# Row gathers and elementwise products on GpSimd beside the second layer of a four-layer graph network

## The chip, the cores and the metric

The kernel runs on one core of a Trainium2 chip. A core has a matrix engine (TensorE, PE in the profile, with PEld for its weight loads), a vector engine (VectorE, DVE), a scalar engine (ScalarE, ACT), a general engine (GpSimd, POOL) and a queue engine (SyncE, SP) that issues most DMAs. Each engine works through its own instructions in order, and they wait for each other through semaphores. The metric is the time on the device, in microseconds, of one execution. Before the change it was 2214.13 us (median of three runs, 2214.03 to 2218.48).

## The reference, cut to what matters

A node matrix x (4096 x 128, float32) goes through four layers. Each computes a graph operation on x and a dense 4096 x 4096 adjacency matrix, adds x, and normalises the rows.

```python
x = _layernorm(x + _L0_gnn_ref(x, adj, adj, L0_gnn_W, L0_gnn_a), axis=-1)
x = _layernorm(x + _L1_gnn_ref(x, adj, L1_gnn_W0, L1_gnn_b0, L1_gnn_W1, L1_gnn_b1), axis=-1)
x = _layernorm(x + _L2_gnn_ref(x, adj, ...), axis=-1)
x = _layernorm(x + _L3_gnn_ref(x, adj, L3_gnn_W_self, L3_gnn_W_neigh), axis=-1)
```

Layer 1, the second, is where the change lies. It is two Chebyshev convolutions with an ELU after each:

```python
def cheb_conv(x, L, W, b):
    Tx0 = x
    out = Tx0 @ W[0]
    Tx1 = L @ x
    out = out + Tx1 @ W[1]
    for k in range(2, W.shape[0]):
        Tx2 = 2.0 * (L @ Tx1) - Tx0
        out = out + Tx2 @ W[k]
        Tx0, Tx1 = (Tx1, Tx2)
    return out + b
h = elu(cheb_conv(x, L, W0, b0))     # 128 -> 256
h = elu(cheb_conv(h, L, W1, b1))     # 256 -> 128
```

Here L is the adjacency matrix. No layer gathers rows by index: all products are dense.

## The kernel before, in words

**Tiles.** Rows of x are kept in 32 tiles of 128 (NT = 32), the whole of x being one buffer of 128 partitions by 32 by 128. Columns of the transposed products come in 8 blocks of 512 (NB = 8, IB = 512, TB = 4 tiles to a block). The adjacency matrix [...] is read again for each product, in chunks of 1 MB (128 x 4 x 512 float32) by `chunk` (line 128), which SP issues into a pool of five buffers, `ld`.

**Layer 1.** The kernel orders the Chebyshev terms into four products with the adjacency matrix. `propagate` (the matmul is line 664) runs the first three: for each of 8 blocks, over 8 chunks and 4 tiles, it adds up one block of 128 x 512 in PSUM.

- First product, with x: ACT copies the block to t1T (line 679), TensorE turns it, VectorE copies it to t1 (line 681).
- Second product, with t1: VectorE makes t2T (line 686), TensorE multiplies by W0 in two halves, and `elu` makes each half of hT: ACT the rectifier (line 651), VectorE the minimum (652), ACT the exponential (653), VectorE the sum of the two parts (654). TensorE then multiplies hT by a weight (line 695), and VectorE copies the result to v (line 697).
- Third product, with v: ACT copies the block (line 709), TensorE turns it, VectorE copies it to w (line 711), ACT puts a product of hT into xT (line 715).
- The fourth product, with w, is written together with layer 2 (line 1126). Its block ends (`block_end`) begin with VectorE at lines 749 and 750 and come to GpSimd at line 775, the first GpSimd work after the constants at the start.

**Order.** In layers 0 and 1 a tile framework schedules the instructions of each engine and places the semaphore waits; `keep_in_program_order` holds those that are to stay as written. Buffers of one pool follow each other in the same memory: the buffers of layer 1's pools `l1w` and `l1h` are given up after the third product, and layer 2's buffers come to lie there, so the first writer of a new buffer waits for the last user of the old one. t1, v and w lie in long-lived buffers whose space is also shared by tag: w takes t1's place and layer 2's hc takes v's. From layer 2 on the order is written out by hand.

**Layer 2 on VectorE and GpSimd.** Its elementwise part is shared between the two engines: VectorE makes tau (line 884) and its own share of a second product (lines 890 and 896), GpSimd the rest (lines 891, 892, 897 and 898).

**Just before layer 1.** `normalize_x` gives x its final values on VectorE (line 151) and its transpose on ACT (line 158). ACT also issues the loads of W1A and W1B there (lines 644 and 646).

Of the kernel before, what the change touches and what calls it, by code (L numbers as in the profile page):

```python
# [11 lines left out]
F32 = mybir.dt.float32  # L12
BF16 = mybir.dt.bfloat16
I32 = mybir.dt.int32
AF = mybir.ActivationFunctionType
ALU = mybir.AluOpType
# [3 lines left out]
P = 128  # L20
IB = 512
TB = IB // P
# [11 lines left out]
def adj_resnorm_d4(ctx: ExitStack, tc: tile.TileContext, x_in, xT_in, adj, adjT, w0g, w0gT, a0, w1a, b1a,  # L34
# [7 lines left out]
    nc = tc.nc  # L42
    N, F = x_in.shape
# [17 lines left out]
    x = state.tile([P, NT, F], F32, name="x")  # L61
# [63 lines left out]
    def chunk(pool, src, ib, c, name="chunk", pinned=False):  # L125

        t = pool.tile([P, TB, IB], F32, name=name)
        r = nc.sync.dma_start(t, src[ib, c])
        if pinned:
            tc.keep_in_program_order(r)  # L130
        return t

    def transpose4(pool, name, src, order=lambda r: r):

        p = pool.tile([P, TB, P], F32, name=name)
        for k in range(TB):
            order(nc.tensor.transpose(p[:, k, :], src(k), ident))  # L137
        return p
# [486 lines left out]
    def network(usual):  # L625

        with ExitStack() as whole:
# [3 lines left out]
            with ExitStack() as first, ExitStack() as l1h_pool:  # L631
                ps_acc, ps_tr, ps_mm = [first.enter_context(tc.tile_pool(name=n, bufs=2, space=PSUM, reuse_waits="tile"))
                                        for n in ("ps_acc", "ps_tr", "ps_mm")]
                if not usual:
                    layer0_general(ps_acc, ps_tr, ps_mm)
                    finished = list(range(NB))
                ld = enter(name="ld", bufs=5)
                if usual:
                    finished = layer0(ld, ps_acc, ps_tr, ps_mm)
                dv = state.tile([96, N], BF16, name="dv")  # L640
                l1w = l1h_pool.enter_context(tc.tile_pool(name="l1w", bufs=2, reuse_waits="tile"))
                l1h = l1h_pool.enter_context(tc.tile_pool(name="l1h", bufs=1, reuse_waits="tile"))
                W1A = l1h.tile([P, 3, HID], F32, name="W1A")
                nc.scalar.dma_start(W1A, w1a.rearrange("k p f -> p k f"))
                W1B = l1h.tile([P, 3 * HH, F], F32, name="W1B")
                nc.scalar.dma_start(W1B, w1b.rearrange("k (h p) f -> p (k h) f", p=P))

                def elu(dst, p, bias):
                    r = l1w.tile([P, IB], F32, name="elu_r")
                    n = l1w.tile([P, IB], F32, name="elu_n")  # L650
                    nc.scalar.activation(r, p, AF.Relu, bias=bias)
                    nc.vector.tensor_scalar(n, p, bias, 0.0, op0=ALU.add, op1=ALU.min)
                    nc.scalar.activation(n, n, AF.Exp)
                    nc.vector.scalar_tensor_tensor(dst, n, -1.0, r, op0=ALU.add, op1=ALU.add)

                def propagate(stationary, order=range(NB), beside=None):


                    for ib in range(NB):
                        p = ps_acc.tile([P, IB], F32, name="pacc")  # L660
                        for n, c in enumerate(order):
                            a = chunk(ld, adjT, ib, c)
                            for k in range(TB):
                                nc.tensor.matmul(p, stationary(c * TB + k), a[:, k, :], start=n == 0 and k == 0,  # L664
                                                 stop=n == NB - 1 and k == TB - 1)
                            if beside and n == 0:
                                beside(p, ib)
                        yield ib, slice(ib * IB, (ib + 1) * IB), p

                t1 = state.tile([P, NT, F], F32, name="t1", tag="yn")  # L670
                t1T = l1h.tile([P, N], F32, name="t1T")
                hT = l1h.tile([P, HH, N], F32, name="hT")
                wd = l1h.tile([P, HH, F], F32, name="wd")
                nc.vector.tensor_sub(wd, W1B[:, 0:HH, :], W1B[:, 2 * HH:3 * HH, :])
                w2x = l1h.tile([P, HH, F], F32, name="w2x")
                nc.vector.tensor_scalar_mul(w2x, W1B[:, 2 * HH:3 * HH, :], 2.0)

                for ib, blk, p in propagate(lambda jt: x[:, jt, :], finished):
                    nc.scalar.copy(t1T[:, blk], p)
                    q = transpose4(ps_tr, "ptr", lambda k: t1T[:, (ib * TB + k) * P:(ib * TB + k + 1) * P])  # L680
                    nc.vector.tensor_copy(t1[:, ib * TB:(ib + 1) * TB, :], q)

                v = state.tile([P, NT, F], F32, name="v")
                for ib, blk, p in propagate(lambda jt: t1[:, jt, :]):
                    t2T = l1w.tile([P, IB], F32, name="t2T")
                    nc.vector.scalar_tensor_tensor(t2T, p, 2.0, xT[:, blk], op0=ALU.mult, op1=ALU.subtract)
                    for hh in range(HH):
                        ph = ps_mm.tile([P, IB], F32, name="pmm")
                        for k, r in enumerate((xT[:, blk], t1T[:, blk], t2T)):
                            nc.tensor.matmul(ph, W1A[:, k, hh * P:(hh + 1) * P], r, start=k == 0, stop=k == 2)  # L690
                        elu(hT[:, hh, blk], ph, B1A[:, hh:hh + 1])
                    q = ps_tr.tile([P, TB, F], F32, name="ptr")
                    for k in range(TB):
                        for hh in range(HH):
                            nc.tensor.matmul(q[:, k, :], hT[:, hh, (ib * TB + k) * P:(ib * TB + k + 1) * P],
                                             w2x[:, hh, :], start=hh == 0, stop=hh == HH - 1)
                    nc.vector.tensor_copy(v[:, ib * TB:(ib + 1) * TB, :], q)


                w = state.tile([P, NT, F], F32, name="w", tag="yn")  # L700
                h0T = xT

                def times_w1(p, ib):
                    for hh in range(HH):
                        nc.tensor.matmul(p, W1B[:, HH + hh, :], hT[:, hh, ib * IB:(ib + 1) * IB], start=False, stop=False)

                for ib, blk, p in propagate(lambda jt: v[:, jt, :], beside=times_w1):
                    lvT = l1w.tile([P, IB], F32, name="t2T")
                    nc.scalar.copy(lvT, p)
                    q = transpose4(ps_tr, "ptr", lambda k: lvT[:, k * P:(k + 1) * P])  # L710
                    nc.vector.tensor_copy(w[:, ib * TB:(ib + 1) * TB, :], q)  # L711
                    ph = ps_mm.tile([P, IB], F32, name="pmm")
                    for hh in range(HH):
                        nc.tensor.matmul(ph, wd[:, hh, :], hT[:, hh, blk], start=hh == 0, stop=hh == HH - 1)
                    nc.scalar.copy(h0T[:, blk], ph)

# [325 lines left out]
            with tc.manual_schedule(engines={mybir.EngineType.PE, mybir.EngineType.DVE, mybir.EngineType.Activation,  # L1044
# [68 lines left out]
                for ib in range(NB):  # L1113
                    early = ib == 1
                    p = ps_nd.tile([P, IB], F32, name="num") if early else ps_p.tile([P, IB], F32, name="pp")
# [55 lines left out]
                this, nt, _, tau2 = behind.popleft()  # L1171
# [9 lines left out]
            for _ in layer3_product(this.blocks):  # L1181
                pass

    network(True)
    with tc.If(nc.values_load(flag[0:1, 0:1], min_val=0, max_val=P) != 0):
        network(False)
# [32 lines left out]
```

## Time and profile before

| | |
|---|---|
| median of three runs | 2214.13 us (2214.03 to 2218.48) |
| span of the profiled execution | 2213.3 us (no other time of that execution is given) |
| TensorE busy | 2139.9 us, 97% |
| VectorE busy | 1186.3 us, 54% |
| GpSimd busy | 857.6 us, 39% |
| ScalarE busy | 562.4 us, 25% |
| first product of layer 1 (line 664 with x) | from 324.1 us; t1 copies at 357.5 to 553.1 us |
| second product | v copies at 590.9 to 830.9 us |
| third product | w copies at 858.0 to 1077.9 us |
| first block end of the fourth product (line 749) | 1106.3 us |
| first GpSimd work after the constants (line 775) | 1115.7 us |
| 1 MB chunk, from issue to landing | 4.9 us (median) |

The times are microseconds from the start of the span. A row of the slices gives the busy share of an engine in tenths, in 40 equal parts of the span. A group line gives the source line, the engine, the operation, what it writes and reads and how often, then its busy time in all and the mean of one in nanoseconds, then the idle time of the engine before it and what ended that. A line of the timeline gives the start, the duration, the engine and the instruction. A line of the windows gives a stretch and its length, the busy time of each engine in it, the clock granted to TensorE, the busy share of the DMA engines and the GB/s that they moved. Instructions that only issue a DMA are not counted as busy.

### The profile page before, as it was taken

To read this page: it belongs to the slowest core of one execution; us is meant where nothing else is said; L and a number is where in the kernel's file an instruction comes from. 1 tells how busy PE (TensorE), PEld (TensorE's weight loads), DVE (VectorE), ACT (ScalarE), POOL (GpSimd) and SP (SyncE) were. 2 spreads that over 40 slices of the span, in tenths; PEclk is the share of its full clock that TensorE was granted. 3 is DMA by queue.
4 is the path that set the end of the run, shared out by engine and by line. 5 is a ranking of instruction groups with operands and counts; after the bars stand their busy time and mean duration, and the time that the engine had idled before them with its cause. 6 is when DMAs were issued, how large, how long until landed. Compare 5 with 4: busy or idle time off the path is not lost. (4 is left out here: it accounts for less than half of the span.)

```text
span 2213.3 us, 22997 instructions
## 1 busy us (share of the span) xinstructions
PE 2139.9 (97%) x8644; PEld 850.8 (38%) x8644; DVE 1186.3 (54%) x1832; ACT 562.4 (25%) x1014; POOL 857.6 (39%) x539
## 2 busy tenths in 40 slices
PE   8999999999999999999999999979999899989997
PEld 3444454444444444444443333322222222333333
DVE  5655460000010110000026877899999999999995
ACT  6755100000000000000043223245333433332213
POOL 0000000000000000000004766698999999999980
PEclk9999999999999999999999999999999999999999
DMA  9886658888767677778876556525666566635545
GB/s 395 334 326 226 228 195 287 300 299 302 265 229 266 230 242 266 262 261 274 283 251 241 195 203 232 209 77 180 247 239 238 183 249 244 228 121 202 191 166 179
DMA packets 87145, 528.18 MB, mean 239 GB/s; under 512 B 9328, under 2 KB 15472, under 8 KB 25712
## 3 DMA queue, kind: packets, MB, share of 16 engines
q1 hardware_dynamic: 80288, 521.64, 66.8%
q10 hardware_dynamic: 6736, 4.98, 0.7%
q8 instruction: 70, 1.15, 0.2%
q14 instruction: 51, 0.42, 0.1%
HBM read 524.49 MB, written 2.10 MB: 238 GB/s over the span
## 5 line engine op out<-in xcount | busy, mean ns | idle before, releaser
L884 DVE SCALAR_TENSOR_TENSOR tau<-D,es,a 128x1024 f32<-128x1024 f32 (+1 forms) x640 | 646.4, 1058 | 44.0 <-ACT a L856 24.8
L892 POOL TENSOR_TENSOR tau<-tau,chunk 128x1024 f32<-128x1024 f32 x192 | 459.2, 2392 | 12.6 <-DVE tau L884 11.7
L775 POOL TENSOR_TENSOR x<-x,B2R 128x512 f32<-128x512 f32 x8 | 10.2, 1276 | 1145.5 <-PE px L137 1145.5
L908 PE MATMUL num<-tau,hc 128*32 128x512 f32 x2048 | 333.9, 606 | 15.0 <-POOL tau L892 9.0
L908 PE MATMUL den<-tau,cs 128*32 128x512 f32 x2048 | 343.6, 597 | 3.3 <-DVE tau L884 0.8
L999 PE MATMUL pp<-chunk,xT 128*128 128x512 f32 (+1 forms) x488 | 232.9, 607 | 0.0
L856 ACT ACTIVATE a<-chunk 128x1024 f32<-128x1024 f32 x160 | 164.2, 1026 | 254.8 <-DVE tau L890 195.1
L664 PE MATMUL pacc<-chunk,t 128*128 128x512 f32 x512 | 223.5, 592 | 0.0
L664 PE MATMUL pacc<-chunk,v 128*128 128x512 f32 x512 | 222.5, 592 | 0.0
L664 PE MATMUL pacc<-chunk,x 128*128 128x512 f32 x512 | 222.1, 592 | 0.0
L891 POOL TENSOR_TENSOR tau<-tau,chunk 128x320 f32<-128x320 f32 x192 | 167.7, 873 | 120.4 <-DVE tau L884 86.5
L1126 PE MATMUL pp<-chunk,w 128*128 128x512 f32 x448 | 204.3, 598 | 0.8 <-DVE oT L749 0.8
L379 PE MATMUL pacc<-chunk,hw 128*128 128x512 f32 x408 | 188.2, 606 | 2.4 <-DVE numT L407 1.7
L890 DVE TENSOR_TENSOR tau<-tau,a 128x704 f32<-128x704 f32 x186 | 163.1, 877 | 0.0
L898 POOL TENSOR_TENSOR tau<-tau,chunk 128x1024 f32<-128x1024 f32 x64 | 151.8, 2372 | 1.0
L908 PEld LDWEIGHTS num<-tau,hc 128*32 128x32 f32 x2048 | 62.4, 109 | 230.9 <-issue 127.8
L908 PEld LDWEIGHTS den<-tau,cs 128*32 128x32 f32 x2048 | 80.4, 110 | 177.0 <-issue 86.9
L664 PEld LDWEIGHTS pacc<-chunk,v 128*128 128x128 f32 x512 | 97.2, 190 | 122.0 <-issue 122.0
L664 PEld LDWEIGHTS pacc<-chunk,x 128*128 128x128 f32 x512 | 96.3, 190 | 115.8 <-issue 115.8
L664 PEld LDWEIGHTS pacc<-chunk,t 128*128 128x128 f32 x512 | 96.1, 190 | 115.3 <-issue 115.3
L999 PEld LDWEIGHTS pp<-chunk,xT 128*128 128x128 f32 x488 | 85.8, 190 | 133.1 <-issue 130.5
L711 DVE COPY w<-ptr 128x512 f32<-128x512 f32 x8 | 5.5, 691 | 241.5 <-PE ptr L137 241.5
(243 smaller groups left out, 1688.6 us busy)
## 6 DMA issues: line engine op xcount, KB each, us to landing
chunk<-in_adjT SPq DMA_DIRECT2D x386, 1024.0 KB, 4.9
chunk<-in_adj SPq DMA_DIRECT2D x80, 1024.0 KB, 5.0
chunk<-in_adj SPq DMA_DIRECT2D x32, 512.0 KB, 4.7
keep<-in_adjT SPq DMA_DIRECT2D x13, 1024.0 KB, 10.0
xT<-in_xT ACTq DMA_DIRECT2D x8, 256.0 KB, 6.6
out<-o ACTq DMA_DIRECT2D x7, 256.0 KB, 2.3
W1A<-in_w1a ACTq DMA_DIRECT2D x1, 384.0 KB, 5.4
W1B<-in_w1b ACTq DMA_DIRECT2D x1, 384.0 KB, 7.4
```

The lines of the kernel that those rows point to most:

```text
L379: in_order(nc.tensor.matmul(p, hw[:, j * TB + k, :], a[:, k, :], start=first and k == 0, stop=last and k == TB - 1))
L664: nc.tensor.matmul(p, stationary(c * TB + k), a[:, k, :], start=n == 0 and k == 0, stop=n == NB - 1 and k == TB - 1)
L775: nc.gpsimd.tensor_tensor(x[:, tb, :], x[:, tb, :], B2R[:, None, :].to_broadcast([P, TB, F]), ALU.add)
L856: nc.scalar.activation(ap, a, AF.Copy, accum_out=deg[:, nt, self.mp:self.mp + 1])
L884: nc.vector.scalar_tensor_tensor(flat(tau[:, q:q + n]), flat(self.D[:, q:q + n]), es[:, nt, head:head + 1], ap, op0=ALU.max, op1=ALU.mult)
L890: nc.vector.tensor_tensor(t2[:, 0:OWN], t[:, 0:OWN], (a if only else ap)[:, 0:OWN], ALU.mult)
L891: nc.gpsimd.tensor_tensor(t2[:, OWN:WB], t[:, OWN:WB], a[:, OWN:WB], ALU.mult)
L892: nc.gpsimd.tensor_tensor(t2[:, WB:2 * WB], t[:, WB:2 * WB], a, ALU.mult)
L898: nc.gpsimd.tensor_tensor(tau2[:, 2:4, :], tau[:, 2:4, :], rep(a, 2), ALU.mult)
L908: nc.tensor.matmul(acc[32 * q:32 * q + 32, :], weights(nt, head, is_den), r[:, q, :], start=nt == 0, stop=nt == NT - 1)
L999: nc.tensor.matmul(p, y[:, c * TB + k, :], a[:, k, lo:lo + n], start=c == blocks[0] and k == 0, stop=end)
L1126: nc.tensor.matmul(p, w[:, c * TB + k, :], a[:, k, :], start=c == 0 and k == 0, stop=c == NB - 1 and k == TB - 1)
```

## The change

In the usual branch, layer 1 copies x to a table in DRAM and makes a list of row indices (31 times the partition, plus a column number). At the end of every block of the first three products GpSimd copies one element of the block's result, which makes it wait for that block. At the ends of blocks 2 to 5 it also gathers rows of the table, 128 rows of 512 bytes to a gather, by indirect DMA into eight buffers in turn, with elementwise products of 128 x 512 between the gathers:

- first product (n = 0): eight gathers in a row, sixteen products, and both once more, to a block;
- second product (n = 1): sixteen times a gather and a product;
- third product (n = 2): eight times a gather and two products.

That is 160 gathers and 256 products in all. Nothing reads the gathered rows or the products.

```diff
                 nc.vector.tensor_scalar_mul(w2x, W1B[:, 2 * HH:3 * HH, :], 2.0)
 
+                if usual:
+                    rows = l1h.tile([P, 32], I32, name="rows")
+                    nc.gpsimd.iota(rows, pattern=[[1, 32]], base=0, channel_multiplier=31)
+                    table = whole.enter_context(tc.tile_pool(name="table", bufs=1, space=bass.MemoryType.DRAM)).tile([N, F], F32, name="table")
+                    nc.scalar.dma_start(table.rearrange("(t p) f -> p t f", p=P), x)
+                    fill = l1h.tile([P, 2, IB], F32, name="fill")
+                    nc.gpsimd.memset(fill, 1.0)
+                count = [0]
+
+                def beside(n, ib):
+                    if ib in (0, 1, 6, 7):
+                        return
+                    for k in range(16 if n < 2 else 8):
+                        gather()
+                        if n == 0 and k % 8 == 7:
+                            for _ in range(16):
+                                pause()
+                        if n > 0:
+                            for _ in range(n):
+                                pause()
+
+
+                def gather(n=P, width=F):
+                    k = count[0] % 8
+                    count[0] += 1
+                    got = l1w.tile([P, F], F32, name="got", bufs=8)
+                    tc.keep_in_program_order(nc.gpsimd.indirect_dma_start(got[0:n, 0:width], None, table if width == F else table[:, 0:width], bass.IndirectOffsetOnAxis(ap=rows[0:n, k:k + 1], axis=0)))
+
+                def pause(n=IB):
+                    tc.keep_in_program_order(nc.gpsimd.tensor_tensor(fill[:, 0, 0:n], fill[:, 0, 0:n], fill[:, 1, 0:n], ALU.mult))
+
+                def after(tile, ib):
+                    tc.keep_in_program_order(nc.gpsimd.tensor_copy(fill[:, 0, 0:1], tile[:, ib * TB, 0:1]))
+
                 for ib, blk, p in propagate(lambda jt: x[:, jt, :], finished):
...
                     nc.vector.tensor_copy(t1[:, ib * TB:(ib + 1) * TB, :], q)
+                    if usual:
+                        after(t1, ib)
+                        beside(0, ib)
...
                     nc.vector.tensor_copy(v[:, ib * TB:(ib + 1) * TB, :], q)
+                    if usual:
+                        after(v, ib)
+                        beside(1, ib)
...
                     nc.scalar.copy(h0T[:, blk], ph)
+                    if usual:
+                        after(w, ib)
+                        beside(2, ib)
```

## The prediction

> **What bounds the kernel now.** I read the engine totals first, then the slices, then each product of layer 1 by windows, and last the waits inside it. On the page of the kernel before:
>
> ```profile
> span 2213.3 us, 22997 instructions
> PE 2139.9 (97%) x8644; PEld 850.8 (38%) x8644; DVE 1186.3 (54%) x1832; ACT 562.4 (25%) x1014; POOL 857.6 (39%) x539
> ...
> POOL 0000000000000000000004766698999999999980
> ...
> DMA  9886658888767677778876556525666566635545
> ...
> q10 hardware_dynamic: 6736, 4.98, 0.7%
> ```
>
> GpSimd (POOL) is idle for the first 20 of 40 slices, so all of layer 1 has it free. The windows of layer 1 (PE, PEld, DVE, ACT and POOL busy, then clock, DMA share and GB/s):
>
> ```profile
> 380.00:414.00 34.00, 34.00 (x86) 15.25 (x85) 1.33 (x2) 1.17 (x2) 0.00 (x0) 1.00 0.89 297
> ...
> 660.00:700.00 40.00, 40.00 (x107) 18.71 (x106) 4.27 (x6) 2.63 (x4) 0.00 (x0) 1.00 0.69 242
> ...
> 920.00:980.00 60.00, 60.00 (x147) 26.95 (x147) 1.38 (x2) 1.77 (x4) 0.00 (x0) 1.00 0.78 265
> ```
>
> TensorE is busy without a gap at full clock in all three products, so layer 1 lasts as long as its matmuls, unless something makes one wait. The DMA engines have 11 to 31% left. In the waits of this stage TensorE waits for no DMA; SP's loads wait for TensorE to free a buffer (204 us in 65 waits from 300 to 560 us).
>
> The timeline at the end of a block of the second product shows the one tight chain:
>
> ```profile
> 689.61 0.63 ACT L653 ACTIVATE elu_n<-elu_n 128x512 f32<-128x512 f32 x1 [0.82 <-DVE elu_n L652]
> ...
> 690.27 0.69 DVE L654 SCALAR_TENSOR_TENSOR hT<-elu_n,elu_r 128x512 f32<-128x512 f32 x1 [0.69 <-ACT elu_n L653]
> ...
> 691.07 0.19 PEld L695 LDWEIGHTS ptr<-w2x,hT 128*128 128x128 f32 x1 [0.24 <-DVE hT L654]
> ```
>
> The ELU's last step, hT, ends at 690.96, and the weight load that needs it starts at 691.07. Behind that load stand all later matmuls, so a late hT makes TensorE late, but for the 0.24 us by which loads run ahead of matmuls.
>
> **What the Trainium skill says.** "SBUF — State Buffer", section "SBUF: two separate sides": VectorE and GpSimd share a port pair as an exclusive lock; a VectorE operation with two SBUF inputs and a GpSimd operation that reads SBUF block each other whole. The trace before agrees. Line 890 reads its second operand mostly from PSUM ("a"), six times from SBUF ("chunk"); in the groups by form:
>
> ```profile
> L890 DVE TENSOR_TENSOR tau<-tau,a 128x704 f32<-128x704 f32 x186 | 163.1, 877 | 0.0
> ...
> L890 DVE TENSOR_TENSOR tau<-tau,chunk 128x704 f32<-128x704 f32 x6 | 7.8, 1292 | 0.0
> ```
>
> and in the timeline:
>
> ```profile
> 1468.23 0.87 POOL L891 TENSOR_TENSOR tau<-tau,chunk 128x320 f32<-128x320 f32 x1
> ...
> 1468.45 1.40 DVE L890 TENSOR_TENSOR tau<-tau,chunk 128x704 f32<-128x704 f32 x1
> ...
> 1469.07 3.00 POOL L892 TENSOR_TENSOR tau<-tau,chunk 128x1024 f32<-128x1024 f32 x1
> ```
>
> VectorE's 877 ns became 1400 beside a GpSimd instruction with 0.65 us left: it lost that less 0.12. The next GpSimd product then took 3.00 us instead of 2.38. "DMA: Bandwidth & Descriptors", section "Issuing engines are not separate DMA queues": GpSimd's DMAs run on the same 16 engines as SP's; no run here shows a GpSimd DMA.
>
> **The change part by part.** Nothing is removed. The orders on TensorE, VectorE and SP are the old ones; ACT gets one DMA issue, GpSimd 442 instructions (160 gathers, 256 products, 24 copies of one element, an iota, a memset) between its constants and line 775. All of them are in the program, although nothing reads the rows gathered.
>
> *Table (2 MB, ACT queue).* It is queued between the last two xT copies (334.7 and 336.4 us) and waits for x, complete at 334, and for the SP chunk that had its semaphore before, issued at 334.40, which lands about 4.9 us later (page, section 6): ACT stands some 4 us, and behind it the last xT copy; the next ACT work is at 356.1. Hidden. It is 4096 rows of 512 B, 256 per engine. Queue q10 used 0.7% of 16 x 2213 us for 6736 packets, 37 ns each: 9.5 us of every engine. Line 646's 768 rows took 7.4 us to land beside the chunks; taking 2 us of it as fixed, 4096 rows take 31 us, so it lands near 370. SP's chunk of 380.6 waits for this semaphore, the first gather comes at 414. Chunks get at most 9.5 - 31 x 0.11 = 6 us later. One chunk takes TensorE 27.94 / 8 = 3.49 us; with five buffers it is needed 14 us after issue and lands in 4.9, so 9 us are spare. Cost 0; every us of landing beyond 380.6 + 9 would cost one.
>
> *GpSimd's length.* A pause is line 775's size, 1.276 us; each waits for the one before, for which its first rows in the timeline show 0.08 (memset to affine select): 1.36. The gather, g, no row shows. Lower end: "SBUF — State Buffer", same section, 0.62 us for a whole small GpSimd DMA. Upper end: "GPSIMD Engine Reference", section "Performance pitfalls for Q7 kernels", 102 cycles for each small read if one is made per index: 128 x 102 / 1.2 GHz = 10.9 us (estimate). I take 1.0, the first-byte time in "DMA: Bandwidth & Descriptors", section "Specifications", which it puts down to emitting descriptors: a row list of 128 needs no more reads than that if they are batched.
>
> - Product one: the third t1 copy is at 413.4. Four blocks of 16 g + 32 pauses: 414 + 64 x 1.0 + 128 x 1.36 = 652.
> - Product two: from the third v copy, 659.5, 64 x (1.0 + 1.36) = 151: 810.
> - Product three: the third w copy is at 920.8; a block takes 8 x 1.0 + 16 x 1.36 = 29.8, under the blocks' 31.4, so the last, from 1015.1, ends at 1045.
>
> Who waits for GpSimd: the first w copy (858, for the last read of t1, done by 652); line 749's oT (1106.3), whose buffer now lies over gathered rows and waits for four gathers; rn, hc, tau and GpSimd's own line 775 (1115.7) behind it. At g = 1.0 there are 61 us of cover. From g = 1.92 on GpSimd has no gap left, and oT, with all of layer 2 behind it on VectorE, is late from 414 + 256 x 1.36 + 160 g = 1106: g = 2.15. Beyond it each 0.1 us of g costs 16 us.
>
> *DMA of the gathers.* 8 rows per engine x 37 ns = 0.3 us. In product one 64 of them take 19 us of 238, 8%, on a share of 0.89; a burst of eight takes 2.4 us of about 8, and with 11% free puts chunks 1.5 us late, against 9 spare. Cost 0.
>
> *The port.* This one is not hidden. hT has two SBUF inputs, twice in each of eight blocks of product two. Pauses fill 174/238 = 73% of GpSimd until 652, and 1.36/2.36 = 58% from 659 to 810. In block one two hT fall in the first stretch; block two's (653, 656) fall between; blocks three to six have eight in the second; block seven (825, 828) is free; block zero has up to 1 us of slack. Hits: 2 x 0.73 + 8 x 0.58 = 6.1. A hit costs half a pause less 0.12, 0.52 us: 3.2 us on VectorE. The second hT of a block has 0.24 us of slack and the shift that the first made; I let 70% reach TensorE: 2.2 us. None of it is won back, since layer 2 starts from the last matmul. Bounds: 0 if the two engines miss each other; if every hT of seven blocks hits a full pause, about 7 x (1.16 + 0.72) = 13.
>
> Sum: 2213.3 + 2.2 = 2215.5 of span. The page gives no other time of the profiled execution; the median of the runs, 2214.13, lies 0.8 above the span. Forecast 2216.4.
>
> **The rivals.**
>
> *GpSimd is late for layer 2.* One mechanism: g above 2.15, and line 749 waits for the gathers. Speaks for it: 10.9 us if the indices are read one by one; against: the 1 us first-byte figure and the cover of 61 us. At g = 3 the time is 2214 + 160 x 0.85 = 2350; at 10.9, about 3600. Slower from g = 2.18 on.
>
> *The gathers hold the port too.* Then GpSimd holds it nearly all the time, and about 12 hT lose 0.5 us each, some whole gathers: 6 us on VectorE, 4 to 9 on TensorE with the second effects: 2218 to 2224. The skill limits the lock to operations that read SBUF; a gather reads only indices.
>
> *Nothing at all.* Pauses and hT miss each other, or the wait is absorbed: 2213.5 to 2215.
>
> *The DMA engines give out.* In product one (0.89) short rows from random places could cost much more than the 37 ns of rows in order; at four times that, 0.3 becomes 1.2 us, a third of the engines in product one, and TensorE waits for chunks: 0.21 x 138 us less the 9 spare, 20 us, 2234. Against: x, loaded in the same 512 B rows, 2 MB, landed in 13 us beside the chunks.
>
> **How the numbers follow.** The port costs 1 to 4.4 us: 0.45. Nothing: 0.13. The port costs more, by gathers that hold it or by luck: 0.23. GpSimd late: 0.12. DMA: 0.05. Faster than the measurement can tell has no mechanism: 0.02. A measurement of this kernel tells about 0.2%, 4.4 us, from no change: same 0.58, slower 0.40, faster 0.02. Low is 2213, the time before less its spread below the median and about 1 us; high, 2226, holds the port's upper bound of 13 us and leaves out the late GpSimd and most of the DMA case. With no change and the port's first case alone the range is 2213.5 to 2218.5.
>
> **What would show it.** hT (line 654) should have a mean of about 0.9 us instead of 693 ns, only in blocks where GpSimd is in products, and the loads of line 695 should wait for it; the last w copy should come at 1080 instead of 1077.9, with everything after it as before. GpSimd should be idle from about 1045, and gathers in product one should follow each other at about 1 us. I am wrong if oT waits for a DMA near 1106, if TensorE waits for chunks between 340 and 660, or if hT is stretched beside gathers.

## The result, and the profile after

The changed kernel takes 2218.97 us (median of 18 runs, 2216.67 to 2221.24), the kernel before 2214.14 us (18 runs, 2212.51 to 2218.48). The ratio is 1.0021, with a 95% interval of 1.0014 to 1.0027: 4.8 us slower, on the edge of the 0.2% that the prediction named as the limit of what can be told from no change. The forecast was 2216.4 us. The profiled execution of the changed kernel took 2221.24 us, the slowest of its 18, for a span of 2219.3 us. So spans of single executions are not compared below; what is compared is the time from the first to the last block inside one product of layer 1.

The page of the changed kernel, in the lines that answer to those of before:

```profile
span 2219.3 us, 23487 instructions
PE 2143.8 (97%) x8644; PEld 850.3 (38%) x8644; DVE 1196.1 (54%) x1832; ACT 562.9 (25%) x1014; POOL 1349.7 (61%) x981
...
POOL 0000000488899980388004766698999999989980
...
DMA  9886659999868777788876556625666566635545
...
q0 software_dynamic: 5120, 10.50, 1.5%
q10 hardware_dynamic: 10848, 7.08, 1.0%
```

GpSimd now works from the eighth slice to the nineteenth, with one idle slice between, and is idle again in the next two, before layer 2 needs it. VectorE is busy 9.8 us longer although it got no instruction. The gathers have their own queue, q0: 10.5 MB, 1.5% of the DMA engines. The windows of layer 1 (PE, PEld, DVE, ACT and POOL busy, clock, DMA share, GB/s):

```profile
380.00:414.00 34.00, 34.00 (x87) 15.25 (x86) 1.38 (x2) 1.17 (x2) 0.37 (x2) 1.00 0.88 299
660.00:700.00 40.00, 39.74 (x105) 18.42 (x104) 5.91 (x7) 2.63 (x4) 36.81 (x37) 1.00 0.74 254
920.00:980.00 60.00, 59.85 (x146) 26.52 (x145) 1.38 (x2) 2.34 (x4) 49.70 (x44) 1.00 0.81 279
```

In the second product VectorE's 4.27 us became 5.91, and TensorE, without a gap before, shows one. The timeline where the prediction showed the tight chain (the same block, the fourth of the second product; before, its second hT began at 690.27):

```profile
688.07 1.28 POOL L707 TENSOR_TENSOR fill<-fill 128x512 f32<-128x512 f32 x1
...
688.62 1.28 DVE L654 SCALAR_TENSOR_TENSOR hT<-elu_n,elu_r 128x512 f32<-128x512 f32 x1 [0.70 <-ACT elu_n L653]
...
689.50 1.26 POOL L704 DMA_INDIRECT got<-table,rows  x1 [0.16 <-issue]
...
690.02 0.30 PEld L732 LDWEIGHTS ptr<-w2x,hT 128*128 128x128 f32 x2 [1.06 <-issue]
...
690.79 1.28 POOL L707 TENSOR_TENSOR fill<-fill 128x512 f32<-128x512 f32 x1
...
691.26 1.36 DVE L654 SCALAR_TENSOR_TENSOR hT<-elu_n,elu_r 128x512 f32<-128x512 f32 x1 [0.70 <-ACT elu_n L653]
```

Both hT come while a GpSimd product runs, and take 1.28 and 1.36 us instead of 0.69: the product ends at 689.35, hT 0.55 later at 689.90. The weight loads (now line 732) stood 1.06 us before the first that needs it. All sixteen hT (line 654), before and after, and who waited for them after:

```profile
L654 DVE SCALAR_TENSOR_TENSOR hT<-elu_n,elu_r x16: 691/693/693, 584.9 to 827.9; 128x512 f32<-128x512 f32 x16
...
L654 DVE SCALAR_TENSOR_TENSOR hT<-elu_n,elu_r x16: 693/1365/1727, 584.4 to 831.2; 128x512 f32<-128x512 f32 x16
...
  PEld ptr L732: 3.4, 7
  PE ptr L732: 2.1, 5
```

Minimum, median and maximum are 693, 1365 and 1727 ns; before they were 691, 693 and 693. The v copies at the ends of the blocks, before (line 697) and after (line 734):

```profile
L697 DVE COPY v<-ptr x8: 690/692/692, 590.9 to 830.9; 128x512 f32<-128x512 f32 x8
...
L734 DVE COPY v<-ptr x8: 691/692/692, 590.4 to 834.5; 128x512 f32<-128x512 f32 x8
```

They span 240.0 us before and 244.1 us after. This is nearly the whole of the loss that layer 1 shows: the t1 copies of the first product span 195.6 us in both kernels, the w copies of the third 220.2 us (220.0 before), and the first oT comes at 1110.2 instead of 1106.3, 3.9 us later. The medians differ by 4.8 us, with an interval from 3.1 to 6.0, so 3.9 us can be all of it.

GpSimd's gathers:

```profile
L704 POOL DMA_INDIRECT got<-table,rows x160: 941/988/1265, 414.5 to 1046.9; - x160
```

### The profile page after: what moved, and what is told of

Its sections match the earlier page's. It is cut to its first block, busy times and chain, and to the rows that moved or that the text cites. A ratio compares the mean times of both kernels' runs of the same rounds, so it can differ in the third digit from the quotient of the medians.

```text
span 2219.3 us, 23487 instructions
## 1 busy us (share of the span) xinstructions
PE 2143.8 (97%) x8644; PEld 850.3 (38%) x8644; DVE 1196.1 (54%) x1832; ACT 562.9 (25%) x1014; POOL 1349.7 (61%) x981
## 5 line engine op out<-in xcount | busy, mean ns | idle before, releaser
L707 POOL TENSOR_TENSOR fill<-fill 128x512 f32<-128x512 f32 x256 | 327.2, 1278 | 13.9
L704 POOL DMA_INDIRECT got<-table,rows x160 | 158.6, 991 | 35.1 <-issue 30.5
```

Of the source, the lines that this page charges most:

```text
L707: tc.keep_in_program_order(nc.gpsimd.tensor_tensor(fill[:, 0, 0:n], fill[:, 0, 0:n], fill[:, 1, 0:n], ALU.mult))
```

## The experiments

Eleven kernels were run. Nothing reads the gathers and products in any of them; what of these a kernel leaves out or alters is said at each. The kernel before, run beside them, had medians of 2214.85 (runs 1 to 4), 2214.21 (5 to 8) and 2214.26 us (9 to 11).

| run | median, us | ratio to before, 95% | hT min/median/max, ns | v copies span, us |
|---|---|---|---|---|
| before | 2214.14 | | 691/693/693 | 240.0 |
| changed | 2218.97 | 1.0021 (1.0014 to 1.0027) | 693/1365/1727 | 244.1 |
| 1 gathers only | 2214.61 | 1.0000 (0.9992 to 1.0008) | 691/692/766 | 240.0 |
| 2 products only | 2215.55 | 1.0004 (0.9996 to 1.0012) | 691/904/1389 | 241.2 |
| 3 elu_r in PSUM | 2214.74 | 1.0001 (0.9993 to 1.0010) | 686/688/689 | 240.0 |
| 4 memsets for products | 2215.28 | 1.0003 (0.9995 to 1.0012) | 691/693/693 | 240.0 |
| 5 work moved off hT | 2215.01 | 1.0005 (0.9997 to 1.0013) | 693/693/693 | 240.0 |
| 6 GpSimd late | 2239.85 | 1.0112 (1.0097 to 1.0128) | 693/1355/1669 | 243.8 |
| 7 shifted by 0.81 us | 2219.93 | 1.0023 (1.0015 to 1.0031) | 693/1378/2023 | 244.9 |
| 8 long products | 2220.81 | 1.0027 (1.0016 to 1.0037) | 692/1438/3083 | 247.9 |
| 9 memset after the gather | 2217.05 | 1.0013 (1.0006 to 1.0020) | 692/693/1801 | 240.3 |
| 10 memset before the gather | 2219.67 | 1.0022 (1.0012 to 1.0031) | 691/1128/2424 | 243.5 |
| 11 before, elu_r in PSUM | 2214.51 | 1.0001 (0.9992 to 1.0009) | 686/687/690 | 240.0 |

My theory was that a product and hT block each other. Its rivals were that the gathers block hT, that the DMA engines give out, that any GpSimd work beside hT does it, and that something outside layer 1 costs the time. The expectations of the first four runs speak of 1.1 us outside the span. That was a mistake of mine: I had set the span of before's profiled execution against the median of others. Wherever one execution's time and span are both known they lie 1.75 to 2.03 us apart, with gathers or without (2221.24 and 2219.3 in the changed kernel, 2214.94 and 2213.1 in run 2, which has none).

**1. Gathers only.** All 256 products are left out, and the gathers, now 400, follow each other without a pause; in product two they run in all blocks.

```diff
-                    if ib in (0, 1, 6, 7):
+                    if n == 0 and ib < 2 or n == 2 and ib in (0, 1, 6, 7):
...
-                    for k in range(16 if n < 2 else 8):
+                    for k in range((24, 28, 8)[n]):
                         gather()
-                        if n == 0 and k % 8 == 7:
...
-                                pause()
```

> The products between the gathers are left out, and gathers run back to back, so that one is under way at every hT: 24 a block in blocks 2 to 7 of product one, 28 a block in all blocks of product two, 8 a block as before in product three. Theory (only GpSimd's products hold the port against hT): hT stays at 693 ns in all 16 blocks, the v copies span 240.0 us as in the kernel before, and the time is the kernel before plus the 1.1 us that the changed kernel shows between its span and its time beyond the 0.8 of before: 2215.2 us (2214 to 2216.5). Rival (a gather holds the port too): hT is 0.2 to 0.5 us longer in most blocks, the v copies span 242 to 245 us, time 2217 to 2221. Rival (DMA): at one gather each 1.15 us in product one TensorE waits there for chunks; the t1 copies then span more than their 195.6 us.

Measured: ratio 1.0000, v copies 240.0 us, hT 0.77 us at most, with a gather under way at every one. The window of run 1 in which gathers alone run beside the first product:

```profile
413.00:552.00 139.00, 139.00 (x339) 61.97 (x338) 3.42 (x5) 2.93 (x5) 105.75 (x115) 1.00 0.96 351
```

The DMA engines are busy to 0.96 and move 351 GB/s, and TensorE still has no gap: 139.00 of 139.00 us. So neither the gathers' transfers nor the gathers on GpSimd cost anything that can be told here. The rivals "the gathers hold the port too" and "the DMA engines give out" fall.

**2. Products only.** The table and all gathers are left out; 32, 24 and 16 products stand in a row (in product two 24 to a block instead of 16, so that they reach hT).

```diff
-                    for k in range(16 if n < 2 else 8):
-                        gather()
...
+                    for k in range((32, 24, 16)[n]):
+                        pause()
```

> Table and gathers are left out; the products stay, 32, 24 and 16 in a row to a block, so that in product two GpSimd is in products at the hT of blocks 3 to 6. Theory (the port): each of these hT is 0.3 to 0.7 us longer, only the first of a block reaches TensorE, so the v copies span 241 to 243.5 us, and the time is 2215 to 2218 us. If the rest of the changed kernel's loss comes from having a GpSimd DMA queue at all, the distance between span and time is back at 0.8 us, against 1.9 with gathers. Rival (the gathers' transfers slow the kernel): hT is stretched, but the v copies stay at 240.0 us and the time at 2214.

Measured: hT is stretched without a single gather, in blocks 3 to 6 to about 0.92 (first) and 1.37 us (second), and the v copies span 1.2 us more; the time alone, 1.0004 with an interval down to 0.9996, would not tell it from no change. So products alone do it; but they cost 1.2 us, where products between gathers cost 4.1. Here GpSimd is done with a block's 24 products in 33 us and waits 1.6 us for the next v copy, so each block finds hT at the same place in a product: the first hT some 0.4 us before its end, and TensorE loses 0.3 us in each of four blocks (their v copies are 34.7 us apart, 34.40 before).

**3. elu_r in PSUM.** hT's second input is moved out of SBUF; all gathers and products stay.

```diff
+                ps_r = first.enter_context(tc.tile_pool(name="ps_r", bufs=2, space=PSUM, reuse_waits="tile"))
...
-                    r = l1w.tile([P, IB], F32, name="elu_r")
+                    r = ps_r.tile([P, IB], F32, name="elu_r")
```

> The changed kernel with one edit: ACT writes the ELU's rectified part to PSUM, so hT reads only one operand from SBUF; all gathers and products stay. Theory (the port, through two SBUF inputs): all 16 hT take 693 ns, the v copies span 240 us, time 2215.2 us (2214 to 2216.5). Rival (the loss comes from somewhere else, transfers or GpSimd's writing): the v copies still span 243 us or more and the time stays at 2218 to 2220 us.

The sixteen hT of run 3 (line 655 there):

```profile
L655 DVE SCALAR_TENSOR_TENSOR hT<-elu_n,elu_r x16: 686/688/689, 585.2 to 828.1; 128x512 f32<-128x512 f32 x16
```

None is stretched, the v copies span 240.0 us, and the time is that of before within 0.1%. The six hT of blocks 0 to 2 carry the proof: each runs beside a product. In blocks 3 to 6, without the waits ahead of them, hT falls within 0.2 us of a gather's beginning, 0.8 to 1.1 us before the next product, and meets none. One buffer's place takes off the cost, so nothing but this clash costs more than 0.1% in the changed kernel.

**11. The control for it:** the same edit on the kernel before.

> The kernel before with elu_r in a PSUM pool and nothing beside the products: a control for the run that did this to the changed kernel. If moving elu_r is worth nothing by itself, the time is that of the kernel before within 0.1 per cent (2213 to 2216) and the v copies span 239.9 to 240.1 us; then the 4 us that the same edit took off the changed kernel were the port's. If it is a gain by itself (a shorter hT, 0.69 us or less, on TensorE's path), the time is 2209 to 2212 and the port's share of the 4 us is smaller by that.

Measured: 1.0001, v copies 240.0 us. The edit alone is worth nothing that can be told, so run 3's gain over the changed kernel is the port's share.

**4. Memsets for products.** Each product becomes a GpSimd memset of 128 x 1024 (0.95 us), which writes and reads nothing.

```diff
-                    tc.keep_in_program_order(nc.gpsimd.tensor_tensor(fill[:, 0, 0:n], fill[:, 0, 0:n], fill[:, 1, 0:n], ALU.mult))
+                    tc.keep_in_program_order(nc.gpsimd.memset(fill, 1.0))
```

> The changed kernel with each product replaced by a memset of 128 x 1024 (0.94 us), a GpSimd operation that writes and does not read; gathers stay. Theory as the skill words it (only a GpSimd operation that reads SBUF blocks a VectorE operation with two SBUF inputs): hT stays at 693 ns, time 2215.2 us (2214 to 2216.5). Rival (any GpSimd operation on SBUF holds the port): several hT are up to 0.8 us longer, the v copies span 241 to 243 us, time 2216 to 2219 us.

Measured: hT 693 ns at most, v copies 240.0 us, although memsets run beside hT in blocks 0, 1 and 3 to 6. This is what the Trainium skill says in "SBUF — State Buffer", section "SBUF: two separate sides": a VectorE operation with two SBUF inputs is held only against a GpSimd operation that reads SBUF. Runs 3 and 4 show both halves of that sentence.

**5. The same work elsewhere.** 161 gathers and 259 products, spread over blocks 0 to 6 of all three products, so that each block's share is done before its hT.

```diff
-                    if ib in (0, 1, 6, 7):
+                    if ib == NB - 1:
...
+                    gathers, pauses = ((8, 12), (8, 10), (7, 15))[n]
+                    for k in range(pauses):
+                        if k < gathers:
+                            gather()
+                        pause()
```

> As much work (161 gathers, 259 products) placed elsewhere: blocks 0 to 6 of each product, 8 gathers and 12 products to a block in product one, 8 and 10 in product two (some 24 us from the v copy, over before the next hT, 27 us after it), 7 and 15 in product three. Theory (the port, at the moment of hT alone): at most the last products reach hT; all or nearly all 16 hT at 693 ns, the v copies span 240.0 us, time as the kernel before, 2214 to 2216 us. Rival (so much GpSimd work and so many gathers cost something wherever they stand): 2218 to 2220 us.

Measured: all sixteen hT take 693 ns, v copies 240.0 us. The amount of work is not what costs; where it stands is.

**6. GpSimd made late.** Four products instead of two behind each gather of product three.

```diff
-                            for _ in range(n):
+                            for _ in range((0, 1, 4)[n]):
```

> The changed kernel with four products after each gather of product three instead of two, so that GpSimd works some 218 us from the third w copy (925 us) to about 1143 us. Theory (layer 2's first buffer waits for the gathers that lie under it): the first oT starts at about 1139 us instead of 1110, all of layer 2 shifts with it, time 2247 us (2240 to 2252). Rival (nothing in layer 2 needs the gathered rows' place so early, or TensorE has other work to do meanwhile): 2219 to 2225 us.

Measured: 2239.85 us, a hair under the expected range. The first oT of run 6 and what it waited for:

```profile
L792 DVE TENSOR_TENSOR oT<-pp,xT x7: 690/691/692, 1129.0 to 1451.8; 128x512 f32<-128x512 f32 x7
...
  DMA got<-table,rows: 47.0, 1
```

It waits for the gathers, the last issued at 1126.3, and comes at 1129.0 where the changed kernel had 1110.2: 18.8 us later, and the time is 20.9 us longer. So the rival "GpSimd is late for layer 2" works as described, with its cost passed on about one to one; I had put the wait ten us too long because I reckoned 1.41 us to a product, where four in a row take 5.30 us.

**7. All of product two's work shifted** by one memset of 0.81 us ahead of its first gather.

```diff
+                        if ib == 2:
+                            tc.keep_in_program_order(nc.gpsimd.memset(fill[:, :, 0:428], 1.0))
```

> The changed kernel with one memset of 0.8 us before the first gather of product two, nothing taken away: GpSimd's beat of a gather and a product (2.43 us) then stands 0.8 us later against the hT of blocks 3 to 6, which in the changed kernel start 0.4 to 0.5 us into a product. Theory (the loss is set by where hT falls in the beat): the first hT of these blocks falls in a gather, hT is stretched less or not at all, the v copies span 241 to 243 us instead of 244.1, time 2215 to 2217.5 us. Rival (hits at random, or a toll of the work as such): the v copies span 243.5 to 245 us, time 2218 to 2220 us.

This expectation was wrong: 244.9 us, no less than without the shift. The start of the fourth block in run 7:

```profile
687.22 0.99 POOL L704 DMA_INDIRECT got<-table,rows  x1 [0.16 <-issue]
688.04 2.02 DVE L654 SCALAR_TENSOR_TENSOR hT<-elu_n,elu_r 128x512 f32<-128x512 f32 x1 [0.70 <-ACT elu_n L653]
688.22 1.29 POOL L707 TENSOR_TENSOR fill<-fill 128x512 f32<-128x512 f32 x1
```

The shift did put hT into a gather, 0.18 us before the product. Yet hT did not go first: it ended at 690.06, 0.55 after the product. And in the next block it is back at 0.44 us into a product, as in the changed kernel. Two questions followed: why hT lost, and why the shift was forgotten within one block.

**8. Long products.** In product two, ten gathers to a block with one difference of 128 x 1024 (a buffer less itself) behind each (1.90 us measured) instead of sixteen gathers with products of 1.28 us.

```diff
-                    for k in range(16 if n < 2 else 8):
+                    for k in range((16, 10, 8)[n]):
...
+                        if n == 1:
+                            pause(2 * IB)
...
+                    if n > IB:
+                        flat = fill.rearrange("p q i -> p (q i)")
+                        tc.keep_in_program_order(nc.gpsimd.tensor_tensor(flat, flat, flat, ALU.subtract))
+                        return
```

> In product two ten gathers and ten products of 128 x 1024 (2.37 us each, a difference instead of a product) to a block instead of sixteen of 128 x 512; the rest as in the changed kernel. Theory (hT waits until the running GpSimd instruction ends): the longest hT takes more than 2.0 us, at most 0.69 + 2.25 = 2.94; each of blocks 3 to 6 loses 0 to 2.2 us by its place in the beat, so the v copies span 241.4 to 250 us, likeliest 245 to 247, time 2216 to 2225 us. Rival (a fixed toll for each collision): no hT above 1.75 us, v copies at 244 us.

```profile
687.78 0.96 POOL L706 DMA_INDIRECT got<-table,rows  x1 [0.16 <-issue]
688.14 3.08 DVE L654 SCALAR_TENSOR_TENSOR hT<-elu_n,elu_r 128x512 f32<-128x512 f32 x1 [0.69 <-issue]
688.75 1.91 POOL L711 TENSOR_TENSOR fill<-fill 128x1024 f32<-128x1024 f32 x1
```

hT waits to the end of the longer product (690.66, hT ends at 691.22), so there is no fixed toll per clash. The v copies, 247.9 us, lie above the likeliest 245 to 247, and this hT, 3.08 us, is longer than the 2.94 expected at most: more than a whole product and hT together, 1.91 + 0.69. It had started 0.61 us before the product and lost to it all the same. With run 7 this gave a new theory: a product that stands directly behind a gather has the port already while the gather runs.

**9 and 10. Who stands behind the gather.** Both runs put a GpSimd memset of 128 x 40 (0.13 to 0.15 us, it reads nothing) into each step of product two, in run 9 between the gather and its product, in run 10 ahead of the gather. The steps are equally long; what stands behind the gather differs, and with it how soon the product follows.

```diff
                         gather()
+                        if n == 1 and (ib, k) != (2, 0):
+                            tc.keep_in_program_order(nc.gpsimd.memset(fill[:, :, 0:20], 1.0))
```

```diff
+                        if n == 1 and (ib, k) not in ((2, 0), (2, 1)):
+                            tc.keep_in_program_order(nc.gpsimd.memset(fill[:, :, 0:20], 1.0))
                         gather()
```

> A 128x40 memset of about 0.13 us stands between each gather and its product in product two, from the second gather of block 2 on; everything else is as in the changed kernel. GpSimd's step grows from 2.44 to about 2.62 us, so that the first hT of block 3 should fall about 0.4 us into a gather rather than 0.55 us into a product, and thirteen steps with the small copy come to about the 34.3 us of a block, so that it stays near there. Theory of the queued product (a product behind a gather takes the port already while the gather runs; a hT that comes during the gather then waits for the end of the next product, as the 2.02 and 3.08 us of the two runs before suggest): with a memset next in the queue the port is free, both hT of block 3 take 0.69 to 0.80 us, and the v copies span 240.8 to 241.8 us, time about 2216. Rival, the port is held only while a product runs: the same here. Rival, the gather itself holds it: first hT of block 3 about 1.2 us.

> The same 128x40 memsets, but each ahead of its gather, so that the product stands directly behind the gather again; the steps are as long as in the run with the memset between. The first hT of block 3 falls about 0.4 us into a gather again. Theory of the queued product: it waits for the rest of the gather and the product behind it, about 2.4 us instead of 0.69, and TensorE loses about 1.7 us in that block; the v copies span 242.4 to 244.5 us. Rival, the port is held only while a product runs: both hT of block 3 take 0.69 to 0.80 us and the v copies span 240.8 to 241.8 us, as with the memset between. Rival, the gather holds it: about 1.2 us.

The first hT of the fourth block in run 9:

```profile
687.63 0.99 POOL L706 DMA_INDIRECT got<-table,rows  x1
688.07 0.69 DVE L654 SCALAR_TENSOR_TENSOR hT<-elu_n,elu_r 128x512 f32<-128x512 f32 x1 [0.70 <-issue]
688.62 0.15 POOL L693 MEMSET fill<- 128x40 f32 x1
688.85 1.27 POOL L709 TENSOR_TENSOR fill<-fill 128x512 f32<-128x512 f32 x1
```

The same in run 10:

```profile
688.59 1.00 POOL L706 DMA_INDIRECT got<-table,rows  x1
689.02 2.42 DVE L654 SCALAR_TENSOR_TENSOR hT<-elu_n,elu_r 128x512 f32<-128x512 f32 x1 [0.70 <-issue]
689.60 1.28 POOL L709 TENSOR_TENSOR fill<-fill 128x512 f32<-128x512 f32 x1
```

hT starts 0.44 and 0.43 us into a gather. With the memset behind the gather it takes 0.69 us, and so do the other seven hT of blocks 3 to 6, which all begin in a gather; TensorE loses nothing in these blocks (each 34.40 us, as before). With the product behind the gather it takes 2.42 us, and the block 36.05. So the gather itself does not hold hT up; the product that follows it does, although hT started up to 0.61 us earlier (run 8). The head start gains hT nothing: it ends 0.56 us after the product's end, as an hT does that began inside a product.

The pair does not show all of the new theory, since the memset also puts the product later. In run 9 the products begin 0.78 to 1.10 us after hT, which alone takes 0.69 and is over; in run 10 the product begins 0.58 us after hT, which alone would still be running. The last block of run 10 has the product directly behind the gather too, but further off (its second hT; the first is alike):

```profile
831.39 1.00 POOL L706 DMA_INDIRECT got<-table,rows  x1
831.40 0.71 DVE L654 SCALAR_TENSOR_TENSOR hT<-elu_n,elu_r 128x512 f32<-128x512 f32 x1 [0.70 <-ACT elu_n L653]
832.40 1.28 POOL L709 TENSOR_TENSOR fill<-fill 128x512 f32<-128x512 f32 x1
```

hT starts 0.93 (first) and 1.00 us (second) before the product and takes 0.69 and 0.71 us. So the product does not have the port for the whole of the gather: an hT 0.61 us ahead of it still loses, one 0.93 us ahead does not. Nor does a product win from any hT that would still be running. In run 9's second block the first hT starts 0.23 us before a product that stands behind another product; it takes 0.70 us, and that product 1.60 instead of 1.27. The early hold is seen behind gathers alone. How it comes about, and whether a memset between gather and product takes it away or only puts the product off, no run shows.

The v copies of run 9 span 240.3 us, a little under the range expected. Its profiled execution (2215.94 us) is among the faster of its twenty, which reach from 2215.03 to 2220.88, and the median is 0.13% above the kernel before, clear of noise. So these four clean blocks can hardly be what every execution had. That hT fell outside the gathers in others would explain it, but no trace shows it, and the cause stays open.

**Why the shift was forgotten.** The v copies of the changed kernel lie 35.01, 35.01 and 35.05 us apart from block 3 to block 6, those of run 7 35.02, 35.04 and 35.03; before it was 34.40. GpSimd needs 35.00 us from the product in which one block's hT falls (688.07) to that of the next (723.07): fourteen steps of 2.44 us, 0.27 more for each of the two gathers behind a hit hT, and some 0.25 for the copy. An hT that waits always leaves 0.55 us after a product's end, whenever it came. So its next block starts in step with GpSimd, wherever it stood before, and TensorE goes on at GpSimd's pace: 0.6 us a block slower than its own. These blocks hold 2.4 of the 4.1 us; block 1 alone, whose two hT fell into the row of products of product one, holds 1.1. Run 10 shows the same with other steps: after its one long wait the v copies are 34.69 and 34.67 us apart, and GpSimd's products, read off against hT, 34.68.

## Why the prediction was right or wrong

- **Time and sign.** 2216.4 forecast, 2218.97 measured; the wide range held it, the likeliest case's own range (to 2218.5) missed it by half a microsecond. No change had the highest chance, and 0.2% was named as its limit; the interval of 0.14 to 0.27% lies across that line.
- **Where.** Right. The loss of layer 1 is in the second product, on hT and the weight load behind it, and all of it went when hT's second input left SBUF (runs 3 and 11). One sign of being wrong did come, in runs 7, 8 and 10: an hT that starts beside a gather is stretched. It is the product behind the gather that does it, since gathers alone do not (run 1).
- **Table.** The cost, nothing, is right: the t1 copies did not move. Its working is not. ACT was to stand some 4 us at the table's DMA; the last xT copy came 1.67 us behind the one before it in both kernels. The table was to land after some 31 us; where a trace shows its landing (runs 1, 3 and 4) it took 20.7.
- **The gather.** 1.0 us taken, 0.99 measured on GpSimd behind a product and 0.94 behind another gather; neither bound, 0.62 or 10.9, was near. The gaps were too small in the sum: a gather behind a gather comes every 1.25 us, 0.30 of it a gap, where 1.0 had been taken with none. So product one's part ended at 668.4 instead of 652, which also put the two hT of block 2, "between" in the prediction, beside products. Product two's part ended at 829, not 810, and covered block 7's first hT. Product three's ended at 1050.5, 5.5 us later than expected, 3.9 of them because its blocks came that much later.
- **DMA of the gathers.** Right; run 1 shows it with two and a half times as many.
- **The port: the mis-sized term.** The working was 6.1 hits of 0.52 us, 3.2 us on VectorE, and 70% of it, 2.2 us, on TensorE. In the profiled execution 14 of 16 hT were stretched, by 0.69 us on the mean, 9.7 us in all (mean hT 1.30 us, not 0.9), and TensorE lost 4.1 us, 42%. VectorE's loss was three times the forecast and TensorE's not quite twice: that too large a share made up in part for too few hits is luck. Three steps of the working failed. First, the chance of a hit was taken as the share of time in which a product runs, 58%; a product queued behind a gather counts too, and together that is at least (1.28 + 0.61) of 2.44 us, 77%, by run 8. Second, hits were taken as independent with half a product lost; a hit sets the place of the next, so blocks 3 to 6 were hit eight times of eight with nearly the same loss each time. Third, the share on TensorE: a block loses the first hT's excess less some 0.1 us (0.59 to 0.74 against 0.50 to 0.65 in blocks 3 to 6), while the second, stretched by 0.67, hides behind what the first lost and its own slack of 0.24.
- **The last step.** The last w copy came at 1081.8, where 1080 had been expected: the 3.9 us, not 2.2, arrived there unchanged. GpSimd was not late; run 6 shows what it costs when it is.
- **From span to time.** The 0.8 us added was the distance between one execution's span and other executions' median. The distance within one execution is about 1.9, wherever it is known. The forecast is not moved by it, since it amounts to adding 2.2 us to the median.

After 1110 us the profiled execution of the changed kernel lost 2.1 us more against that of before, where both do the same. It was the slowest of its 18 runs, and runs of the kernel before alone differ by 6 us. In the traces of the eleven experiments the same stretch, from the first oT to the end, lasts from 1106.4 us (run 8, where hT waited longest) to 1109.2 (run 7), against 1107.0 before and 1109.1 in the changed kernel; so it does not go with the clash. What these 2.1 us are stays open.

## What to carry to other kernels

In these runs GpSimd work beside a busy TensorE was free as long as no VectorE operation on TensorE's path read two SBUF operands while GpSimd was in an operation that reads SBUF, or within some 0.6 us of one that stood behind a gather. Look for such an operation first, and give it one operand in PSUM, or put the work where that operation does not stand. Do not price such a clash as chance times half an operation: two periodic streams that wait for each other can fall into step, as here in blocks 3 to 6, and then the slower pace is paid in every block. The one shift in time that was tried, 0.81 us, did not cure it.

## What the runs showed that I had not expected

- A GpSimd product directly behind a gather goes ahead of an hT that started before it: hT that started 0.18, 0.58 and 0.61 us before it waited for its end (2.02, 2.42 and 3.08 us), while hT 0.93 and 1.00 us before it did not. The Trainium skill says in "SBUF — State Buffer", section "SBUF: two separate sides", that whichever starts first gets the port; by the recorded starts of these three that is not so, and the measurement decides.
- The blocking goes the other way at the gather's beginning only. A gather that begins while hT holds the port takes 1.26 us instead of 0.99 (up to 1.48 in run 9), while one in which hT begins later stays at 0.99. In run 3, where hT reads one operand from PSUM, a gather that begins 0.02 or 0.07 us after hT takes 0.98. Where a gather begins 0.02 to 0.04 us after hT, hT takes 0.74 to 0.77 us (run 1).
- 2560 packets of 4 KB carried 10.5 MB of gathered 512-byte rows (the other 2560 of q0 have 4 bytes each): eight rows to a packet, 159 ns each at the median, some 20 ns to a row where 37 had been taken.
